# Layer 1 of a spatial convolution scan on Trainium2: the third group's up scan and the fourth group's down scan as joint steps of 256 columns

## The chip, the cores and the metric

The kernel runs on one core of one Trainium2 chip. The metric is the device time of one execution in microseconds. It is float32 throughout. Besides the timed runs there is one profiled execution, whose trace is read here; its times are microseconds from the start of its span.

## What is computed

Two layers of the same kind, each `x = x + scan(groupnorm(x))`, on a tensor of 32 images, 48 channels, 64 rows, 128 columns. A scan goes through all rows downwards, then upwards, then through all columns to the right and to the left; each step adds to the next row (or column) a 1-D convolution (5 taps, 48 to 48 channels) of the row just finished.

```python
def step(w, b):
    def f(carry, inp):
        nxt = inp + _conv1d(carry, w, b)
        return (nxt, nxt)
    return f
xs = jnp.moveaxis(x, 2, 0)
_, d_rest = jax.lax.scan(step(down_w, down_b), xs[0], xs[1:])      # down
D = jnp.concatenate([xs[0][None], d_rest], 0)
seq = jnp.concatenate([D[Hh - 3::-1], D[Hh - 1:Hh]], 0)
_, u_rest = jax.lax.scan(step(down_w, down_b), D[Hh - 1], seq)     # up
...                                                                # right, left
x = x + _L0_conv_ref(_gn(x), ...)
x = x + _L1_conv_ref(_gn(x), ...)
```

The row steps up and down use the same weights (`down_w`). Images do not depend on one another; within an image a step needs the step before it.

## The kernel before

The 32 images are four groups of eight. `PHASES` lists twelve stages in order: a "rows" stage scans one group down and up, a "cols" stage scans two groups to the right and to the left. The four groups are numbered 0 to 3 in the profile's tile names: `step_12u` is a step's sums in layer 1, group 2, going up; `step_13d` is group 3 going down. The stages that matter here are numbers 8 (layer 1, group 2: 12d, then 12u) and 9 (layer 1, group 3: 13d, then 13u); stage 10 is the first column stage of layer 1 (`step_10r`, `step_10l`).

A row (128 columns of 8 images of 48 channels) lies in the arena in SBUF as three blocks `o` of 128 partitions (eight neighbouring columns times 48 channels make 384 partitions) and 128 elements (16 column blocks times 8 images). `row_step` (through `step`, line 881) makes one row: nine products in the order of `PRODUCTS`, each with its own 128x128 weights (some with 96 or 112 columns of weights), sum up in three PSUM tiles; when the last product of a block is issued, one vector operation (line 903) adds the bias and the row that waits there, and writes the new row over it. The first block is complete after the fifth product, the third after the sixth, the second after the ninth; the next step starts with products of the first and the third block.

The arena has three slots of 32 rows. Stage 8 has rows 0 to 31 in slot 0 and rows 32 to 63 in slot 1; stage 9 has rows 0 to 31 in slot 2 and rows 32 to 63 in slot 1 (`slots`, `row_views`), so its second half is loaded when stage 8 has left slot 1. Rows come from DRAM (`take_rows`, from `mid`, written by layer 0's last stage, by 16 rows), are scaled in place by ScalarE (`scale_rows`: group norm's factor and offset) and go, when finished upwards, to DRAM (`move_rows` to `ups`, tile `upb` in the profile), from where the column stages read them (`load_unit`).

What sets the order: an `agenda` of (time, function) entries, times in steps. `plan_rows` and `plan_cols` fill it, and the last loop runs through the steps of all stages, carrying out before each step what has come due. `in_order` chains instructions of one engine in that order, so an agenda's times set the order in each engine's queue; when something really runs is decided by semaphores that the framework derives from the tiles' accesses. Loads and stores here are all issued by SP, in one queue.

Of the kernel before, what the change touches and what calls it, by code (L numbers as in the profile page):

```python
# [41 lines left out]
GB = 8  # L42
# [35 lines left out]
def weight_runs():  # L78
# [35 lines left out]
    ("cols", 1, 0),  # L114
    ("cols", 1, 1),
)


@with_exitstack
def kernel(  # L120
# [567 lines left out]
    def row_views(k):  # L688
        return [slot[i].rearrange("p (o h n) -> p o h n", o=NG, h=HALF) for i in slots(k)]

    def row(k, h):
        return row_views(k)[h // HALF][:, :, h % HALF]

    def move_rows(k, h0, h1, to_dram, q=None):

        _, layer, g = PHASES[k]
        view = row_views(k)[h0 // HALF]
        t = (ups if to_dram else source)[layer][g]
        for h in range(h0, h1, E8):
            end = min(h1, h + E8)  # L700
            for o in range(NG):
                for e, c0, c1, p0 in pieces(o):
                    here = view[p0 : p0 + c1 - c0, o, h % HALF : h % HALF + end - h]
# [12 lines left out]

    def take_rows(k, h0, h1, o):

        _, layer, g = PHASES[k]
        view = row_views(k)[h0 // HALF]  # L720
        for e, c0, c1, p0 in pieces(o):
            here = view[p0 : p0 + c1 - c0, o, h0 % HALF : h0 % HALF + h1 - h0]
            for q in range(NQ):
                dma(
                    here[:, :, q * RUN : (q + 1) * RUN],
                    by_quarter(source[layer][g], e, h0, h1, q)[c0:c1],
                )

    def scale_rows(k, h0, h1, groups=range(NG)):
        _, layer, g = PHASES[k]  # L730
        scale, offset = coeffs[layer, g]
        view = row_views(k)[h0 // HALF][:, :, h0 % HALF : h0 % HALF + h1 - h0]
        view = view.rearrange("p o h (k b) -> p o b h k", b=GB)
        for o in groups:
            for b in range(GB):
                args = view[:, o, b], scale[:, o, b : b + 1], offset[:, o, b : b + 1]
                nc.scalar.activation(  # L737
                    args[0], args[0], AF.Identity, bias=args[2], scale=args[1]
                )

    def scale_at_once(k, h0, h1, eng, o0=0, o1=NG):

        _, layer, g = PHASES[k]
        view = row_views(k)[h0 // HALF][:, o0:o1, h0 % HALF : h0 % HALF + h1 - h0]
        view = view.rearrange("p o h (k b) -> p o (h k) b", b=GB)
        for t, op in zip(coeffs[layer, g], (ALU.mult, ALU.add)):
            t = t[:, o0:o1].unsqueeze(2).to_broadcast([FULL, o1 - o0, (h1 - h0) * NK, GB])
            eng.tensor_tensor(view, view, t, op)
# [129 lines left out]
                dma(in_output(j, half, e)[c0 * NH : c1 * NH], src[at : at + (c1 - c0) * NH])  # L878


    def step(key, weights, b_at, src, inp, dst, whole, part):


        ps = [
            ps_step.tile([FULL, N], F32, tag=f"step{o}", name=f"step{o}_{key}")
            for o in range(NG)
        ]
        left = [sum(1 for p in PRODUCTS if p[1] == o) for o in range(NG)]
        seen = [0] * NG
        for i, o, s in PRODUCTS:  # L890
            seen[o] += 1
            m = COLUMNS.get((i, o, s), FULL)
            at = FULL * (o - NG * s - i + 1)
            nc.tensor.matmul(  # L894
                part(whole(ps[o])[0:m], -s),
                weights[:, i, at : at + m],
                part(src(i), s),
                start=seen[o] == 1,
                stop=seen[o] == left[o],
            )  # L900
            if seen[o] == left[o]:
                layer, way = b_at
                nc.vector.scalar_tensor_tensor(  # L903
                    dst(o),
                    whole(ps[o]),
                    bd[:, o, layer, way : way + 1],
                    inp(o),
                    ALU.add,
                    ALU.add,
                )  # L910

    def row_step(k, h, prev, inp, name):
        _, layer, g = PHASES[k]

        def part(t, s):
            return t[:, max(0, s) * GB : N + min(0, s) * GB]

        step(
            f"{layer}{g}{name}{h}",
            wt[f"down{layer}"],  # L920
            (layer, DOWN),
            lambda i: prev[:, i],
            lambda o: inp[:, o],
            lambda o: row(k, h)[:, o],
            lambda ps: ps,
            part,
        )

    def col_step(k, way, v0, v1):
        _, layer, pair = PHASES[k]  # L930

        def col(v):
            kb, e = divmod(v, E8)
            j, kk = divmod(kb, KQ)
            view = slot[slots(k)[j % 3]].rearrange(
                "p (o m e k b) -> p o e k m b", o=NG, e=E8, k=KQ, b=GB
            )
            return lambda o: view[:, o, e, kk]

# [4 lines left out]
        step(  # L944
            f"{layer}{pair}{'drl'[way]}{v1}",
            wt["right" if way == RIGHT else "left"],
            (layer, way),
            col(v0),
            col(v1),
            col(v1),  # L950
            lambda ps: ps.rearrange("p (m b) -> p m b", b=GB),
            part,
        )

    def scans(k):
        if PHASES[k][0] == "rows":
            for h in range(1, H):
                yield lambda h=h: row_step(k, h, row(k, h - 1), row(k, h), "d")
            end = last.rearrange("p (o n) -> p o n", o=NG)
            for h in range(H - 2, -1, -1):  # L960
                yield lambda h=h: row_step(
                    k, h, row(k, h + 1), row(k, h - 1) if h else end, "u"
                )
        else:
            for v in range(1, W):
                yield lambda v=v: col_step(k, RIGHT, v - 1, v)
            for v in range(W - 2, -1, -1):
                yield lambda v=v: col_step(k, LEFT, v + 1, v)


    agenda = []
# [14 lines left out]
    def plan_input(g, times, work, lag, nats, perms):  # L986
# [5 lines left out]
        for j, t in enumerate(times):  # L992
# [6 lines left out]
                at(t + i * work / per + 4, put_out, g, rows * j + r, perm)  # L999
            at(t + lag, stats.take_others, pieces_of * j, nat)  # L1000
            if j + ahead < len(times):
                free = t + 7
                at(free, take_in, g, rows * (j + ahead), nat)
        spread(t + work + lag + (0, 2, 32, 5)[g], scaling(f"x{g}", 0, g, stats, x_masks, (0, 0, 8, 0)[g]), 1)

    def plan_rows(k, t0, prev):
        if k == 1:
# [5 lines left out]
        if k:  # L1013
            for i in range(4):
                if PHASES[k][1]:
                    for o in range(NG):
# [8 lines left out]
        seam = following and follows(k + 1)  # L1025
        if seam:
            cuts = cuts[2:]
            end = t0 + 2 * (H - 1)
# [13 lines left out]
        at(  # L1042
            t0 + H - 1,
            nc.gpsimd.tensor_copy,
            last.rearrange("p (o n) -> p o n", o=NG),
            row(k, H - 1),
# [7 lines left out]
    def plan_cols(k, t0, prev):  # L1054
# [5 lines left out]
        for i in range(n):  # L1060
# [93 lines left out]
            store_result(k, 0, i, perm)  # L1154


    starts = [0]
    for kind, *_ in PHASES:
        starts.append(starts[-1] + 2 * ((H if kind == "rows" else W) - 1))
    for k, (kind, layer, _) in enumerate(PHASES):  # L1160
        (plan_rows if kind == "rows" else plan_cols)(k, starts[k], PHASES[k - 1][0])

# [217 lines left out]
            in_order(fn, *args)  # L1380

    for k in range(len(PHASES)):
        for one in scans(k):
            catch_up(done)
            in_order(one)
            done += 1
    catch_up(float("inf"))


# [51 lines left out]
```

## Time and profile before

| what | value |
|---|---|
| three timed runs | 4165.12, 4167.84, 4174.18 us |
| median of them | 4167.84 us |
| profiled execution: its span, first to last instruction (no other time of it is listed) | 4158.1 us |
| median less that span | 9.7 us |
| TensorE busy, share of the span | 97% |
| VectorE / ScalarE / GpSimd busy | 52% / 30% / 20% |
| granted TensorE clock, mean | 0.989 |

How to read it: TensorE's matmuls are pipelined, so the profile's "busy" of an instruction says little about its cost; the distance from one matmul to the next does. An idle engine costs only where the others wait for it. A group's row gives the line of the kernel, the engine, the operation, the tiles written and read, the count, then busy time and mean duration of one, then the idle time ahead of them and what ended it.

### The profile page before, as it was taken

The page shows a single profiled execution, that of the slowest core. Times are in us where ns is not written, and L with a number is a line of the kernel's source. Part 1 is how long each engine was busy: PE and PEld are TensorE (multiplying, and loading weights), DVE is VectorE, ACT ScalarE, POOL GpSimd, SP SyncE. Part 2 cuts the span into 40 slices and gives each one's busy share as a digit, 9 for nine tenths or more (in the row PEclk, how much of TensorE's full clock was granted, in tenths as well). Part 3 has the DMA queues.
Part 4 walks back from the last instruction along what each step waited for, and adds up shares of the span by engine and source line. Part 5 has one row for each costly group of instructions (what it writes and reads, how often), then busy time and mean ns, then how long its engine had stood idle before and what let it go on. Part 6 is the DMA issues. An engine that isn't in the chain of part 4 may idle for free. (4 is left out here: it accounts for less than half of the span.)

```text
span 4158.1 us, 90227 instructions
## 1 busy us (share of the span) xinstructions
PE 4049.2 (97%) x36724; PEld 4031.7 (97%) x36724; DVE 2141.6 (52%) x6503; ACT 1251.6 (30%) x2440; POOL 826.1 (20%) x763
## 2 busy tenths in 40 slices
PE   6999999999999999999999999999999999999994
PEld 5999999999999999999999999999999999999994
DVE  6454444456654454444457664444444444444444
ACT  4645000536964543000006863423000002200122
POOL 5630010334222000010013220000000015610353
PEclk9999999999999999999999999999999999999997
DMA  9987769669979999258419979959289029999799
GB/s 299 229 184 121 116 127 214 209 159 252 218 188 163 173 163 156 35 103 194 107 30 273 181 147 145 141 93 150 49 141 208 1 55 247 295 257 155 146 233 197
DMA packets 2208479, 681.08 MB, mean 164 GB/s; under 512 B 2008656, under 2 KB 2157376, under 8 KB 2183488
## 3 DMA queue, kind: packets, MB, share of 16 engines
q1 hardware_dynamic: 2063936, 582.35, 68.4%
q10 hardware_dynamic: 141568, 87.46, 8.8%
q0 software_dynamic: 2560, 5.51, 0.5%
q8 instruction: 289, 4.73, 0.5%
q14 instruction: 126, 1.03, 0.1%
HBM read 398.29 MB, written 295.14 MB: 167 GB/s over the span
## 5 line engine op out<-in xcount | busy, mean ns | idle before, releaser
L829 POOL TENSOR_TENSOR arena<-arena 128x2048 f32<-128x2048 f32 x80 | 362.7, 4545 | 1481.7 <-PE step_10l L894 458.3
L737 ACT ACTIVATE arena<-arena,offset,scale 128x256 f32<-128x256 f32 (+2 forms) x744 | 538.4, 818 | 384.4 <-DMA arena<-mid 206.1
L674 POOL COPY arena<-arena 128x256 f32<-128x256 f32 x340 | 201.0, 659 | 447.6 <-DMA arena<-in_x 418.2
L612 ACT ACTIVATE early<-arena 128x256 f32<-128x256 f32 x192 | 129.7, 675 | 443.0 <-DMA arena<-xin 308.1
L894 PE MATMUL step_00r<-arena,early 128*128 128x128 f32 x2286 | 252.1, 274 | 6.1 <-DMA arena<-arena 5.1
L894 PEld LDWEIGHTS step_00r<-arena,early 128*128 128x128 f32 x2286 | 251.2, 185 | 7.0 <-issue 5.5
L894 PE MATMUL step_01r<-arena,early 128*128 128x128 f32 x2286 | 252.2, 274 | 5.8 <-DMA arena<-arena 4.9
L894 PEld LDWEIGHTS step_01r<-arena,early 128*128 128x128 f32 x2286 | 251.3, 185 | 6.6 <-issue 5.3
L894 PE MATMUL step_11r<-arena,early 128*128 128x128 f32 x2286 | 249.3, 272 | 0.3 <-DVE arena L903 0.3
L894 PEld LDWEIGHTS step_11r<-arena,early 128*128 128x128 f32 x2286 | 248.7, 184 | 0.8 <-DVE arena L903 0.7
L894 PE MATMUL step_00l<-arena,wleft 128*128 128x128 f32 x2286 | 249.2, 272 | 0.0
L894 PEld LDWEIGHTS step_00l<-arena,wleft 128*128 128x128 f32 x2286 | 248.7, 184 | 0.0
L894 PE MATMUL step_10l<-arena,wleft 128*128 128x128 f32 x2286 | 248.5, 272 | 0.0
L894 PE MATMUL step_11l<-arena,wleft 128*128 128x128 f32 x2286 | 248.5, 272 | 0.0
L894 PE MATMUL step_10r<-arena,early 128*128 128x128 f32 x2286 | 248.4, 272 | 0.0
L894 PE MATMUL step_01l<-arena,wleft 128*128 128x128 f32 x2286 | 248.4, 272 | 0.0
L894 PEld LDWEIGHTS step_10l<-arena,wleft 128*128 128x128 f32 x2286 | 248.4, 184 | 0.0
L894 PEld LDWEIGHTS step_11l<-arena,wleft 128*128 128x128 f32 x2286 | 248.4, 184 | 0.0
L894 PEld LDWEIGHTS step_01l<-arena,wleft 128*128 128x128 f32 x2286 | 248.4, 184 | 0.0
L894 PEld LDWEIGHTS step_10r<-arena,early 128*128 128x128 f32 x2286 | 248.4, 184 | 0.0
L297 ACT COPY early<-arena 128x1 f32<-128x1 f32 x2 | 0.4, 192 | 709.9 <-DVE arena L903 709.9
L851 ACT COPY arena<-arena 128x256 f32<-128x256 f32 x172 | 99.6, 656 | 362.4 <-POOL arena L829 256.3
(202 smaller groups left out, 7088.5 us busy)
## 6 DMA issues: line engine op xcount, KB each, us to landing
xin<-arena SPq DMA_DIRECT2D x94, 512.0 KB, 4.3
arena<-in_x SPq DMA_DIRECT2D x18, 2048.0 KB, 11.4
arena<-xin SPq DMA_DIRECT2D x96, 384.0 KB, 10.9
arena<-mid SPq DMA_DIRECT2D x384, 96.0 KB, 3.1
upb<-arena SPq DMA_DIRECT2D x192, 192.0 KB, 3.9
arena<-upb SPq DMA_DIRECT2D x96, 384.0 KB, 11.8
arena<-xin SPq DMA_DIRECT2D x174, 192.0 KB, 4.3
mid<-arena SPq DMA_DIRECT2D x32, 1024.0 KB, 11.2
```

Of the source, the lines that this page charges most:

```text
L297: fn(*args)
L612: nc.scalar.activation(junk[:, 0:n], view[:, b], AF.Identity, accum_out=self.sum[:, i, j : j + 1])
L674: copy(dst[:, r, q], src[:, r0 + r, q])
L737: nc.scalar.activation(args[0], args[0], AF.Identity, bias=args[2], scale=args[1])
L829: eng.tensor_tensor(unit, unit, nat, ALU.add)
L851: copy(by_w(perm)[:, a], src[:, a])
L894: nc.tensor.matmul(part(whole(ps[o])[0:m], -s), weights[:, i, at : at + m], part(src(i), s), start=seen[o] == 1, stop=seen[o] == left[o],)
```

## The change

Stage 9's down scan no longer follows stage 8's up scan: both run together as 63 joint steps. In joint step `i` group 2 makes row 62 - i (upwards) and group 3 makes row 1 + i (downwards). Both use the same weights, so one product streams both rows: 256 columns (240 for the products across a border) in one matmul, taken from two places of the arena by an access pattern with a far stride (`beside`), into PSUM tiles of twice the width. One vector operation finishes both rows of a block. The last joint step, whose upward row takes its input from a kept copy, uses two. In the agenda a joint step counts as two steps, and stage 9's start moves back over stage 8's up scan.

So that group 3 can run while group 2 is still in slot 1, its rows lie in the arena in blocks of eight in reversed order (`place`): its rows 32 to 39 lie where group 2's rows 56 to 63 were, which are finished first. Each block is loaded once the rows before have been stored: `take_rows` and `scale_rows` for group 3 go by eight rows, 34 and 17 half steps ahead of their use, and group 2's stores go one half step behind the row they need. Stage 10 loads its first quarter 58 instead of 70 steps ahead.

```diff
+JOINED = (9,)
...
+    def rows_at(k, h0, h1):
+        places = sorted(place(k, h) for h in range(h0, h1, E8))
+        at = places[0] * E8 + h0 % E8
...
-    def step(key, weights, b_at, src, inp, dst, whole, part):
+    def step(key, weights, b_at, src, inp, dst, whole, part, turn=lambda t: t):
         ps = [
-            ps_step.tile([FULL, N], F32, tag=f"step{o}", name=f"step{o}_{key}")
+            ps_step.tile([FULL, 2 * N], F32, tag=f"step{o}", name=f"step{o}_{key}")
...
-                part(whole(ps[o])[0:m], -s),
+                part(turn(whole(ps[o]))[0:m], -s),
                 weights[:, i, at : at + m],
-                part(src(i), s),
+                part(turn(src(i)), s),
...
+                to, sums, term = dst(o), whole(ps[o]), inp(o)
+                todo = [(to, sums, term)]
+                if isinstance(term, tuple):
+                    todo = [(to[:, c], sums[:, c], term[c]) for c in range(len(term))]
+                for to, sums, term in todo:
+                    nc.vector.scalar_tensor_tensor(
+                        to, sums, bd[:, o, layer, way : way + 1], term, ALU.add, ALU.add
+                    )
...
+    def beside(a, b):
+        shift = b.offset - a.offset
+        assert a.ap == b.ap and shift > 0
+        return bass.AP(a.tensor, a.offset, [a.ap[0], (shift, 2), *a.ap[1:]])
...
+            lambda i: both(row(ku, hu + 1), row(kd, hd - 1), i),
+            inp,
+            lambda o: both(row(ku, hu), row(kd, hd), o),
...
+        if k in JOINED:
+            for i in range(H // E8):
+                h, t = i * E8, t0 + 2 * i * E8
+                for o in range(NG):
+                    at(t - 34 + 2 * o, take_rows, k, h, h + E8, o)
+                at(t - 17, scale_rows, k, h, h + E8)
...
-            t = t0 + 2 * (H - 1) - h0
+            t = t_up + up * (H - 1 - h0)
             if k == 0:
                 t += 16 if h0 >= HALF else 68
+            elif up == 2:
+                t += 1
             elif not following:
-                t = t0 + 92 + 5 * (H - h1) / E8 + (34 if h1 <= HALF else 0)
+                t = t_up + 29 + 5 * (H - h1) / E8 + (34 if h1 <= HALF else 0)
             at(t, move_rows, k, h0, h1, True)
...
-                early = 30 if after else 46 if k == 2 else 70
+                early = 30 if after else 46 if k == 2 else 58 if k - 1 in JOINED else 70
```

What this makes of the engines' queues stands in the built programs. In their rows a number behind a tile's name tells the tiles apart, the sizes at the end are those of the operand written. TensorE first, the third to the eighth product of group 2's first step upwards, before:

```order
L894 MATMUL step2_12u62_24965<-arena_72,early_73 96x120
L894 MATMUL step0_12u62_24963<-arena_72,early_73 96x120
L894 MATMUL step0_12u62_24963<-arena_72,early_73 128x128
L894 MATMUL step2_12u62_24965<-arena_72,early_73 128x128
L894 MATMUL step1_12u62_24964<-arena_72,early_73 128x128
L894 MATMUL step1_12u62_24964<-arena_72,early_73 112x128
```

and the same place now, where `12u62d1` is group 2's row 62 together with group 3's row 1:

```order
L917 MATMUL step2_12u62d1_25121<-arena_72,early_73 96x15x2x8
L917 MATMUL step0_12u62d1_25119<-arena_72,early_73 96x15x2x8
L917 MATMUL step0_12u62d1_25119<-arena_72,early_73 128x16x2x8
L917 MATMUL step2_12u62d1_25121<-arena_72,early_73 128x16x2x8
L917 MATMUL step1_12u62d1_25120<-arena_72,early_73 128x16x2x8
L917 MATMUL step1_12u62d1_25120<-arena_72,early_73 112x16x2x8
```

The products, their order and their weights are the same; the width went from 128 to 16x2x8 and from 120 to 15x2x8 elements. Group 3's own nine products for row 1, which stood 63 steps further on, are gone.

VectorE, with the semaphores that an instruction waits for in brackets (`DMAHW0` to `DMAHW7` count DMAs that have landed, the others what an engine has finished): group 2's rows 55 and 54 upwards, before:

```order
L903 SCALAR_TENSOR_TENSOR arena_72<-step0_12u55_25080,bd_75,arena_72 128x128 [waits PE_49]
L903 SCALAR_TENSOR_TENSOR arena_72<-step2_12u55_25082,bd_75,arena_72 128x128 [waits DVE_49,PE_49]
L903 SCALAR_TENSOR_TENSOR arena_72<-step1_12u55_25081,bd_75,arena_72 128x128 [waits DVE_49,PE_49]
L903 SCALAR_TENSOR_TENSOR arena_72<-step0_12u54_25095,bd_75,arena_72 128x128 [waits PE_49]
L903 SCALAR_TENSOR_TENSOR arena_72<-step2_12u54_25097,bd_75,arena_72 128x128 [waits DVE_49,PE_49]
L903 SCALAR_TENSOR_TENSOR arena_72<-step1_12u54_25096,bd_75,arena_72 128x128 [waits DVE_49,PE_49]
```

and the joint steps of rows 55 and 8, 54 and 9, and the first two operations of 53 and 10 now:

```order
L931 SCALAR_TENSOR_TENSOR arena_72<-step0_12u55d8_25248,bd_75,arena_72 128x2x128 [waits DMAHW3_49,DMAHW4_49,DMAHW2_49,DMAHW5_49,DMAHW1_49,DMAHW6_49,DMAHW0_49,DMAHW7_49,PE_49,Activation_49]
L931 SCALAR_TENSOR_TENSOR arena_72<-step2_12u55d8_25250,bd_75,arena_72 128x2x128 [waits DMAHW3_49,DMAHW2_49,DMAHW4_49,DMAHW1_49,DMAHW5_49,DMAHW0_49,DMAHW6_49,DVE_49,DMAHW7_49,PE_49,Activation_49]
L931 SCALAR_TENSOR_TENSOR arena_72<-step1_12u55d8_25249,bd_75,arena_72 128x2x128 [waits DVE_49,PE_49]
L931 SCALAR_TENSOR_TENSOR arena_72<-step0_12u54d9_25313,bd_75,arena_72 128x2x128 [waits DMAHW4_49,DMAHW3_49,DMAHW5_49,DMAHW2_49,DMAHW6_49,DMAHW1_49,DMAHW7_49,DMAHW0_49,PE_49]
L931 SCALAR_TENSOR_TENSOR arena_72<-step2_12u54d9_25315,bd_75,arena_72 128x2x128 [waits DVE_49,PE_49]
L931 SCALAR_TENSOR_TENSOR arena_72<-step1_12u54d9_25314,bd_75,arena_72 128x2x128 [waits DVE_49,PE_49]
L931 SCALAR_TENSOR_TENSOR arena_72<-step0_12u53d10_25340,bd_75,arena_72 128x2x128 [waits PE_49]
L931 SCALAR_TENSOR_TENSOR arena_72<-step2_12u53d10_25342,bd_75,arena_72 128x2x128 [waits DVE_49,PE_49]
```

Rows 55 and 54 waited for TensorE and VectorE alone. Now group 3's row 8, the first of a newly loaded block, brings DMA semaphores and ScalarE's (which scales the block) to step 55; and the first operation of step 54 has DMA semaphores without ScalarE's. The same stands at steps u46d17, u38d25, u30d33, u22d41, u14d49 and u6d57, each one step behind the place where group 2 has finished eight rows.

SP, around group 2's first store (`upb2`, ten DMAs for eight rows) and the loads of group 3 (`arena<-mid3`), before:

```order
L286 DMA arena_72<-mid3_86 16x16x32 x4
L286 DMA arena_72<-mid3_86 48x16x32 x8
L286 DMA arena_72<-mid3_86 32x16x32 x4
L286 DMA upb2_93<-arena_72 48x32x32 x2
L286 DMA upb2_93<-arena_72 32x32x32
L286 DMA upb2_93<-arena_72 16x32x32
L286 DMA upb2_93<-arena_72 48x32x32 x2
L286 DMA upb2_93<-arena_72 16x32x32
L286 DMA upb2_93<-arena_72 48x32x32 x2
L286 DMA upb2_93<-arena_72 32x32x32
L286 DMA upb2_93<-arena_72 48x32x32 x2
L286 DMA upb2_93<-arena_72 32x32x32
```

and now:

```order
L287 DMA arena_72<-mid3_86 48x8x32 x8
L287 DMA arena_72<-mid3_86 32x8x32 x4
L287 DMA upb2_93<-arena_72 48x32x32 x2
L287 DMA upb2_93<-arena_72 32x32x32
L287 DMA upb2_93<-arena_72 16x32x32
L287 DMA upb2_93<-arena_72 48x32x32 x2
L287 DMA upb2_93<-arena_72 16x32x32
L287 DMA upb2_93<-arena_72 48x32x32 x2
L287 DMA upb2_93<-arena_72 32x32x32
L287 DMA arena_72<-mid3_86 16x8x32 x4
L287 DMA arena_72<-mid3_86 48x8x32 x8
L287 DMA arena_72<-mid3_86 16x8x32 x4
```

Before, loads of group 3's rows 0 to 31 (by 16 rows) end, and then the stores of rows 56 to 63, 48 to 55 and so on follow one another. Now ten stores stand between loads of eight rows each: the stores of rows 56 to 63 come behind loads for group 3's rows 24 to 31, and the rest of that block's loads behind them.

More of the change, by code (lines that the diff above doesn't have):

```diff
@@ L700, in move_rows @@
             end = min(h1, h + E8)
+            view = rows_at(k, h, end)
             for o in range(NG):
                 for e, c0, c1, p0 in pieces(o):
-                    here = view[p0 : p0 + c1 - c0, o, h % HALF : h % HALF + end - h]
+                    here = view[p0 : p0 + c1 - c0, o]
                     if to_dram:
@@ L719, in take_rows @@
         _, layer, g = PHASES[k]
-        view = row_views(k)[h0 // HALF]
+        turned = h1 - h0 > E8 and place(k, h0) > place(k, h0 + E8)
+        if turned:
+            for h in range(h0, h1, E8):
+                take_rows(k, h, h + E8, o)
+            return
+        view = rows_at(k, h0, h1)
         for e, c0, c1, p0 in pieces(o):
-            here = view[p0 : p0 + c1 - c0, o, h0 % HALF : h0 % HALF + h1 - h0]
+            here = view[p0 : p0 + c1 - c0, o]
             for q in range(NQ):
@@ L924, in row_step, with lines, two_row_step, both @@
             lambda o: row(k, h)[:, o],
-            lambda ps: ps,
+            lambda ps: ps[:, 0:N],
             part,
+        )
+    def beside(a, b):
+        shift = b.offset - a.offset
+        assert a.ap == b.ap and shift > 0
+        return bass.AP(a.tensor, a.offset, [a.ap[0], (shift, 2), *a.ap[1:]])
+    def lines(t):
+        return t.rearrange("p (m b) -> p m b", b=GB)
+    def two_row_step(ku, hu, kd, hd):
+        _, layer, g = PHASES[ku]
+        first = slots(ku)[0] < slots(kd)[0]
+        def both(u, d, o):
+            u, d = lines(u[:, o]), lines(d[:, o])
+            return beside(*((u, d) if first else (d, u)))
+        def inp(o):
+            if hu:
+                return both(row(ku, hu - 1), row(kd, hd), o)
+            pair = lines(last.rearrange("p (o n) -> p o n", o=NG)[:, o]), lines(row(kd, hd)[:, o])
+            return pair if first else pair[::-1]
+        def part(t, s):
+            return t[:, max(0, s) : NK + min(0, s)]
+        step(
+            f"{layer}{g}u{hu}d{hd}",
+            wt[f"down{layer}"],
+            (layer, DOWN),
+            lambda i: both(row(ku, hu + 1), row(kd, hd - 1), i),
+            inp,
+            lambda o: both(row(ku, hu), row(kd, hd), o),
+            lambda ps: ps.rearrange("p (c m b) -> p c m b", c=2, b=GB),
+            part,
+            lambda t: t.rearrange("p c m b -> p m c b"),
         )
@@ L1001, in plan_input @@
             if j + ahead < len(times):
-                free = t + 7
-                at(free, take_in, g, rows * (j + ahead), nat)
-        spread(t + work + lag + (0, 2, 32, 5)[g], scaling(f"x{g}", 0, g, stats, x_masks, (0, 0, 8, 0)[g]), 1)
+                at(t + 7, take_in, g, rows * (j + ahead), nat)
+        t += work + lag + (0, 2, 32, 5)[g]
+        spread(t, scaling(f"x{g}", 0, g, stats, x_masks, (0, 0, 8, 0)[g]), 1)
     def plan_rows(k, t0, prev):
+        down, up = (2 if k in JOINED else 1), (2 if k + 1 in JOINED else 1)
+        t_up = t0 + down * (H - 1)
         if k == 1:
@@ L1027, in plan_rows @@
             cuts = cuts[2:]
-            end = t0 + 2 * (H - 1)
+            end = t_up + up * (H - 1)
             at(end - E8, move_rows, k, E8, 2 * E8, True, 0)
@@ L1154, in last_results @@
             store_result(k, 0, i, perm)
-    starts = [0]
-    for kind, *_ in PHASES:
-        starts.append(starts[-1] + 2 * ((H if kind == "rows" else W) - 1))
+    starts, end = [], 0
+    for k, (kind, *_) in enumerate(PHASES):
+        n = (H if kind == "rows" else W) - 1
+        starts.append(end - 2 * n if k in JOINED else end)
+        end = starts[-1] + (2 if k in JOINED else 1) * n + (2 if k + 1 in JOINED else 1) * n
     for k, (kind, layer, _) in enumerate(PHASES):
@@ L1382 @@
     for k in range(len(PHASES)):
-        for one in scans(k):
+        for units, one in scans(k):
             catch_up(done)
             in_order(one)
-            done += 1
+            done += units
     catch_up(float("inf"))
```

50 lines of the change are left out of this document (27 added, 23 removed).

## The prediction

> **What bounds the kernel now.** I read the page's head and its busy times first, then the stages of layer 1's third and fourth row phases (windows), then the matmuls by form.
>
> ```profile
> span 4158.1 us, 90227 instructions
> PE 4049.2 (97%) x36724; PEld 4031.7 (97%) x36724; DVE 2141.6 (52%) x6503; ACT 1251.6 (30%) x2440; POOL 826.1 (20%) x763
> ```
>
> TensorE and its weight loads are busy 97% of the span; nothing else passes 52%. So a change pays only where it makes TensorE's stream denser, and costs wherever TensorE waits. Now the two stages that the change joins, 12u (third group up) and 13d (fourth group down), and 13u after them:
>
> ```profile
> core 0: us, PE busy (x) PEld busy (x) DVE busy (x) ACT busy (x) POOL busy (x), PEclk, DMA share, GB/s
> 2733.30:2857.80 124.50, 124.50 (x1137) 124.50 (x1136) 60.65 (x190) 34.41 (x46) 0.50 (x1) 1.00 0.69 109
> 2857.80:2983.00 125.20, 125.20 (x1136) 124.75 (x1135) 60.89 (x190) 1.95 (x3) 0.00 (x0) 1.00 0.55 95
> 2983.00:3107.50 124.50, 124.50 (x1137) 124.50 (x1136) 60.64 (x190) 0.00 (x0) 0.51 (x1) 1.00 0.69 117
> ```
>
> 63 steps take 124.5 us, 1.976 us each: nine products of two instructions, 109.8 ns apart. TensorE idles nowhere, the granted clock is 1.00, and weight loading fills the whole stretch as well. 13d's extra 0.7 us are its waits for loaded rows. The two stages take 124.5 + 125.2 = 249.7 us; that is all the change can touch directly.
>
> **The change, part by part: the matmuls.** 63 joint steps of nine products take the place of 126 steps: half the weight loads, products twice as wide. Does a wide product cost less than two narrow ones? Nothing here has 256 columns, so I bound it by the rows of 128 and of 512 columns.
>
> ```profile
> L894 PE MATMUL step_12u<-arena,early x1134: 266/275/304, 2733.4 to 2857.8; 128*128 128x128 f32 x126, 128*96 128x120 f32 x63
> L1299 PE MATMUL rows<-arena,wleft x40: 592/592/1222, 19.6 to 38.1; 128*128 128x512 f32 x40
> 23.60:37.50 13.90, 13.90 (x34) 6.19 (x33) 1.00 1.01 417
> ```
>
> From 128 to 512 columns an instruction lasts 592 - 275 = 317 ns longer, 0.826 ns a column, so 128 columns stream in 106 ns of the 109.8 ns pace. In the window of 512-column products the weight loads are busy 6.19 of 13.90 us, against all of the time in the steps: wide products hide their weight loads. A 256-column product thus needs 211 ns an instruction (everything beyond the streaming hidden) to 219.6 (nothing gained). I take 215.5, the streaming plus the 4 ns left over now, since at 512 columns the pace is 13.90/33 = 421 ns, no better than streaming alone; for the border products (240 columns) 202. A joint step is then 14 x 0.2155 + 4 x 0.202 = 3.83 us, 63 of them 241 us: **8 us less** than 249.7 (bounds 0 and 13). Eight blocks of loaded rows instead of four in 13d add about another 0.7 us of such waits: net 7.
>
> **The wait that the change adds.** The VectorE rows shown above carry the case. In the joint scan the first vector operation of steps u54d9, u46d17, u38d25, u30d33, u22d41, u14d49 and u6d57 waits for DMA semaphores on top of TensorE; for u30d33 the second one does, too. Before, no step of 12u or 13u waits for a DMA. What are these DMAs? Not the fourth group's rows: those are waited for at u55d8, with ScalarE's semaphore (they are scaled there), and at u54d9 ScalarE is not waited for. What stands on SP just ahead is the ten stores of third-group rows 56 to 63, which SP can issue only once the row above them is done. One vector operation now writes two rows that lie 11392 to 13184 elements apart (`beside`), and the stored rows lie between the two in the arena; I read the wait as the framework guarding the span between the rows, not as a value that is needed. It is in the program whatever its reason, and it repeats every eight steps, seven times.
>
> What is queued behind it: VectorE's two other operations of that step, and through them TensorE's next step, whose first product reads what the waiting operation writes. Behind TensorE waits the whole kernel. What the store takes comes from 13u, where the same ten stores run alone:
>
> ```profile
> L286 SPq DMA_DIRECT2D upb<-arena x10: 302/842/1362, 3028.2 to 3036.0; - x10
> DMA to landing us min/median/max: 2.9/3.7/4.2
> ...
> 3028.00:3030.00 2.00, 2.00 (x21) 2.00 (x20) 0.99 (x4) 0.00 (x0) 0.00 (x0) 1.00 0.41 72
> 3030.00:3039.00 9.00, 9.00 (x85) 9.00 (x84) 4.65 (x15) 0.00 (x0) 0.00 (x0) 1.00 1.00 161
> 3039.00:3040.00 1.00, 1.00 (x12) 1.00 (x11) 0.28 (x2) 0.00 (x0) 0.00 (x0) 1.00 0.03 4
> ```
>
> Issues from 3028.2 to 3036.0, the last one landing 3.7 us later: 11.5 us, during which the 16 DMA engines are full. In 13u nobody waits for it; TensorE is busy throughout. Bounds from the stores that run in a queue of 40, and from their fastest rows:
>
> ```profile
> L286 SPq DMA_DIRECT2D upb<-arena x40: 433/774/2287, 2634.0 to 2673.7; - x40
> DMA to landing us min/median/max: 3.0/3.9/5.4
> L903 DVE SCALAR_TENSOR_TENSOR arena<-step_12u,bd,arena x186: 341/351/352, 2734.7 to 2856.1; 128x128 f32<-128x128 f32 x186
> ```
>
> Ten at 0.774 us and 3.0 to land make 10.7; ten at 39.7/39 = 1.02 us and 3.9 make 14.1. Set 0 where the first joint step ahead of the wait ends on TensorE. Its first bank is finished four products earlier (8 x 0.2155 = 1.7 us); with the matmul's own latency (275 ns + 106) and the vector operation, the first store issues at about -1.0. The vector operation over 256 columns lies between 0.351 (as now) and 0.702 (two of the present ones); I take 0.5, and it adds little either way. The last store lands at -1.0 + 11.5 = 10.5, the waiting operation ends at 11.0, and TensorE starts the next step there instead of at 3.83. **Stall 7.2 us**, seven times: 50 (from 10.7: 45; from 14.1: 68).
>
> **The clock.** Such a stall is long enough to lower TensorE's clock. Three stalls in this trace are alike; one with its surroundings, and the resumptions after the other two:
>
> ```profile
> 1850.34 2.01 PE L894 MATMUL step_01r<-arena,early 128*128 128x128 f32 x7 [4.92 <-DMA arena<-arena]
> ...
> 1845.30:1850.30 5.00, 0.12 (x2) 0.00 (x0) 0.35 (x1) 0.00 (x0) 0.00 (x0) 0.88 0.10 14
> 1850.30:1855.90 5.60, 5.56 (x25) 5.41 (x26) 1.05 (x3) 0.00 (x0) 0.00 (x0) 0.50 0.10 14
> 1855.90:1861.50 5.60, 5.60 (x53) 5.60 (x52) 2.77 (x9) 0.00 (x0) 0.00 (x0) 1.00 0.09 12
> 577.40:582.80 5.40, 5.40 (x25) 5.22 (x26) 1.05 (x3) 0.00 (x0) 0.00 (x0) 0.50 0.10 14
> 1181.30:1186.90 5.60, 5.51 (x26) 5.55 (x27) 1.29 (x4) 5.38 (x15) 0.17 (x1) 0.50 1.04 365
> ```
>
> After 4.92 us of waiting the clock stands at 0.50 for the next 5.6 us, in which 25 matmuls issue instead of 53: 2.8 us lost. In the stall itself it was low for 0.24 x 5.0 = 1.2 us, 6.8 in all. If the low stretch is as long after a 7.2 us stall, some 3.4 us of it fall behind the stall, 1.7 lost; if it lasts as long after the work resumes, 2.8. I take 2.1 each, 15 us in all (12 to 20). [...]
>
> **What stays hidden.** The fourth group's loads become 320 of 8 rows instead of 160 of 16, all on SP, in the same queue as the stores.
>
> ```profile
> L286 SPq DMA_DIRECT2D arena<-mid x80: 303/527/2032, 2675.2 to 2724.6; - x80
> ...
> 2685.53 6.05 ACT L737 ACTIVATE arena<-arena,offset,scale 128x256 f32<-128x256 f32 x8 [43.56 <-DMA arena<-mid]
> ```
>
> Eighty loads take 49.4 us here, 0.62 us each with their queue; half the rows cost no more, so one block of eight rows is at most 40 x 0.62 = 25 us of SP, and with ten stores 36. Eight joint steps with one stall last 8 x 3.83 + 7.2 + 2.1 = 40 us, so SP keeps up, and each block is asked for 15 to 17 steps ahead of its use. ScalarE's scaling of a block is three times 6.05 us at most, 18 us, in the same 40. The first block: from 2634.0, 20 stores (20 us), its 40 loads (25), 10 more stores between them (10) and the scaling (18) end at 2707, ahead of 2733.3. If this cover fell away, a late block would cost what SP exceeds 40 us by, seven times. The column phase behind loads its first quarter 58 instead of 70 units ahead, 115 us before it is read: no cost.
>
> **Sum.** -7 + 50 + 15 = +58 us. The profiled span of 4158.1 becomes 4216; the median of the runs shown is 9.7 us above that span (4167.84), and I put the same 9.7 us on top: **4226 us**, 1.4% slower.
>
> **Rivals.**
> 1. No stall: if the semaphore values named are those of the loads, which landed long before, the vector operation never waits and the change gives -7 us: 4161. It decides by which DMA was counted last. For it: the rows name a semaphore, not a value. Against it: the wait stands exactly one step behind each eight-row edge of the rows going up, and without ScalarE's. [...] Chance 6%, of it 2% a gain of over 0.2%, 4% within (0.2%, 8 us, is about what a measurement of this kernel can tell from no change).
> 2. A short stall: stores that land within about 5 us, as a single one does (3.7 us after its issue), would hold TensorE some 1 us and leave the clock up: -7 + 7 = 4168. It decides at the DMA engines' rate; the row of 161 GB/s at share 1.00 says they are the limit, so 2%.
> 3. SP becomes the bound: if a load of eight rows holds SP longer than 0.75 us, the block and its stores pass 40 us and each edge gets later still; at 1 us, 10 us more at each of seven: 4296. The issue times above (0.527 median) speak against it: 6%.
> 4. The forecast: 86%.
>
> The range goes from +40 (45 of stall and 8 of clock, the gain at 13) to +83 (68 and 20, the gain at 5): 4208 to 4251, and leaves out rivals 1 to 3 and some of the forecast's edges, about 2 in 10. Faster 0.02, same 0.06, slower 0.92.
>
> **What the changed kernel's profile will show.** Matmuls of 256 columns about 215 ns apart (step 1 is right if a step without a wait takes 3.8 to 3.85 us). Seven gaps on TensorE in some 300 us, about 38 to 42 us apart, and VectorE's idle time there ended by the DMA that writes the third group's store buffer `upb`. PEclk at 0.5 behind each gap. If the gaps are missing, rival 1 holds; if they are ended by `mid` loads or ScalarE, rival 3. If the gaps are there but the clock stays at 1.00, the time is near 4211.

## The result and the profile after

The changed kernel takes **4235.57 us** (median of 5 runs, 4229.78 to 4238.76) against 4167.84: ratio 1.0159, 95% interval [1.0147, 1.0170], 1.6% slower. That is 10 us above the forecast of 4226 and inside its range.

The page of the profile after the change, its head, busy times and two rows of its slices:

```profile
span 4237.1 us, 88135 instructions
PE 4063.6 (96%) x35590; PEld 4003.7 (94%) x35590; DVE 2107.9 (50%) x6317; ACT 1279.3 (30%) x2536; POOL 826.5 (20%) x763
...
PE   6999999999999999999999999987899999999994
...
PEclk9999999999999999999999999998999999999997
```

TensorE has 1134 instructions fewer and yet a longer busy time, and in three slices (27th to 29th, some 320 us) the engine is no longer full; the clock's row drops in one of them, the 28th. Cut by stage and by one of the gaps (columns: stretch, length, busy time and instructions of each engine, granted clock, DMA share, GB/s), the windows of the changed kernel read:

```profile
2749.70:2784.10 34.40, 34.40 (x164) 29.49 (x163) 11.71 (x26) 12.55 (x24) 0.50 (x1) 1.00 0.34 54
2784.10:2791.60 7.50, 0.39 (x2) 0.00 (x1) 0.54 (x2) 0.00 (x0) 0.00 (x0) 0.79 0.86 138
2791.60:2797.00 5.40, 5.40 (x17) 4.34 (x18) 1.64 (x4) 0.00 (x0) 0.00 (x0) 0.66 0.52 81
2797.00:2802.00 5.00, 5.00 (x25) 4.31 (x24) 1.88 (x4) 3.94 (x8) 0.00 (x0) 1.00 0.54 84
...
2749.70:3061.40 311.70, 259.71 (x1137) 217.32 (x1136) 87.73 (x192) 71.14 (x136) 0.50 (x1) 0.90 0.40 64
```

The last row is the whole joint stage: 311.7 us where the two stages of before took 249.7. TensorE idles 311.7 - 259.7 = **52.0 us** of it. The rows above are one of seven such places: nine steps without a gap and the clock at 1.00; 7.5 us with hardly an instruction; then 5.4 us in which 17 matmuls issue where 25 fit in 5.0 us afterwards, at a mean clock of 0.66. The groups of the matmuls by step (last columns: busy us, mean ns, idle us before them and who ended it), three with a gap and one without:

```profile
L917 PE MATMUL step_12u53d<-arena,early 128*128 128x256 f32 x12 | 4.2, 487 | 7.1 <-DVE arena L931 7.1
L917 PE MATMUL step_12u13d<-arena,early 128*128 128x256 f32 x12 | 4.7, 533 | 8.0 <-DVE arena L931 8.0
L917 PE MATMUL step_12u29d<-arena,early 128*128 128x256 f32 x12 | 5.0, 538 | 7.8 <-DVE arena L931 7.8
L917 PE MATMUL step_12u52d<-arena,early 128*128 128x256 f32 x12 | 3.1, 379 | 0.0
```

(The profile drops the digits behind `d`; `12u53d` is step u53d10.) The gaps stand at the first product of steps 53, 45, 37, 29, 21, 13 and 5, each ended by VectorE. What VectorE waited for at the first of them, by the instructions that belong to its tile, and the ten stores beside it:

```profile
L917 PE MATMUL step_12u54d<-arena,early x18: 366/379/379, 2780.5 to 2784.1; 128*128 128x256 f32 x12, 128*96 128x240 f32 x4, 128*112 128x256 f32 x2
L931 DVE SCALAR_TENSOR_TENSOR arena<-step_12u54d,bd,arena x3: 474/474/483, 2791.1 to 2791.9; 128x256 f32<-128x256 f32 x3
its engine sat idle before it (us, times) until:
  DMA arena<-mid: 9.9, 1
...
L287 SPq DMA_DIRECT2D upb<-arena x10: 302/699/1688, 2779.5 to 2787.1; - x10
...
DMA to landing us min/median/max: 2.8/3.7/3.9
```

The stores issue from 2779.5 to 2787.1 and the last lands 3.8 us later, at 2790.9; VectorE starts at 2791.06 and TensorE goes on at 2791.60. But the view names another DMA, a load of group 3 (`arena<-mid`). SyncE issues such loads right behind the stores, and the first of them lands at 2791.2, when VectorE is already at work. Over the whole stage the waits view splits in the same way:

```profile
DVE arena L931 <- DMA arena<-mid: 48.0, 6, 10.2
...
DVE arena L931 <- DMA upb<-arena: 26.0, 3, 10.8
```

So by name six of the nine waits are for loads. But at step 14 (and at step 6) no load lands near the end of the wait, the view names the stores, and the gap is as long as the others:

```profile
L931 DVE SCALAR_TENSOR_TENSOR arena<-step_12u14d,bd,arena x3: 475/476/484, 2994.9 to 2995.7; 128x256 f32<-128x256 f32 x3
its engine sat idle before it (us, times) until:
  DMA upb<-arena: 10.8, 1
```

The built program agrees: at steps 54, 46, 38, 30, 22, 14 and 6 every DMA count that VectorE waits for is the count of a store to `upb2`, none that of a load. The name in the view is that of a neighbour in the queue. The runs below test it.

### The profile page after: what moved, and what is told of

Same layout as the page of the kernel before. It is cut to its first block, busy times and chain, and to the rows that moved or that the text cites. A ratio compares the mean times of both kernels' runs of the same rounds, so it can differ in the third digit from the quotient of the medians.

```text
span 4237.1 us, 88135 instructions
## 1 busy us (share of the span) xinstructions
PE 4063.6 (96%) x35590; PEld 4003.7 (94%) x35590; DVE 2107.9 (50%) x6317; ACT 1279.3 (30%) x2536; POOL 826.5 (20%) x763
## 5 line engine op out<-in xcount | busy, mean ns | idle before, releaser
L760 ACT ACTIVATE arena<-arena,offset,scale 128x256 f32<-128x256 f32 (+2 forms) x840 | 565.9, 767 | 459.3 <-DMA arena<-mid 224.4
```

What stands on the lines that cost most here:

```text
L760: nc.scalar.activation(args[0], args[0], AF.Identity, bias=args[2], scale=args[1])
```

## The experiments

In all of them the joint stage's length, TensorE's idle time in it and its busy time beyond 241.3 us (what the stage takes where nothing waits, as in e1; the half clock, added products and slower restarts are in it) come from one windows row, the time from 4 to 12 runs each. The runs of before that stand beside them have medians of 4170.15 (e1 to e4) and 4167.61 us (e5 to e8).

| kernel | time, us | ratio to before [95%] | joint stage | TensorE idle | busy beyond |
|---|---|---|---|---|---|
| the change | 4235.57 | 1.0159 [1.0147, 1.0170] | 311.7 | 52.0 | 18.4 |
| e1 two writes | 4161.13 | 0.9978 [0.9967, 0.9989] | 241.3 | 0 | 0 |
| e2 not joined | 4168.41 | 0.9999 [0.9989, 1.0009] | - | - | - |
| e3 32 products in the gap | 4259.63 | 1.0214 [1.0194, 1.0233] | 337.9 | 0 | 96.6 |
| e4 one step split | 4201.66 | 1.0075 [1.0059, 1.0092] | 281.6 | 26.9 | 13.4 |
| e5 16 products in the gap | 4218.24 | 1.0120 [1.0106, 1.0134] | 298.9 | 5.9 | 51.7 |
| e6 stores two steps later | 4233.52 | 1.0154 [1.0140, 1.0168] | 311.4 | 52.4 | 17.7 |
| e7 stores of four rows | 4160.28 | 0.9982 [0.9973, 0.9990] | 241.2 | 0 | 0 |
| e8 two steps split | 4167.34 | 1.0000 [0.9991, 1.0009] | 245.4 | 2.9 | 1.2 |

### e1: two rows, two writes

```diff
-            if hu:
-                return both(row(ku, hu - 1), row(kd, hd), o)
-            pair = lines(last.rearrange("p (o n) -> p o n", o=NG)[:, o]), lines(row(kd, hd)[:, o])
+            up = row(ku, hu - 1) if hu else last.rearrange("p (o n) -> p o n", o=NG)
+            pair = lines(up[:, o]), lines(row(kd, hd)[:, o])
             return pair if first else pair[::-1]
```

> Every joint step writes its two rows by two VectorE operations of 128 columns per row block (six a step in place of three); matmuls, order of the steps, loads and stores stay. Theory (VectorE waits because the write of two far rows spans the rows that are being stored, and no value is late): the seven TensorE gaps vanish, the clock stays 1.00 in the joint stage, a joint step takes 3.83 to 3.85 us throughout, the stage 242 us instead of 311.7; time 4236 - 54 (gaps) - 15 (half clock) = 4161 to 4170 us, within 0.2% of before or a little faster. Rival A (the rows wait for the stores by need, or the stores hold up something else): gaps of 7 us stay, 4230 to 4240. Rival B (the six shorter operations are themselves too slow for a step, about 6 x 0.35 us = 2.1 us of 3.83, with the sums' buffer single): 0.2 us more a step, no gaps of 7 us, 4175 to 4185.

The joint stage of e1 in the windows, the matmuls of a step that had a gap, and its six vector operations:

```profile
2740.10:2981.40 241.30, 241.30 (x1136) 206.88 (x1135) 110.03 (x377) 71.15 (x136) 0.50 (x1) 1.00 0.51 82
...
L917 PE MATMUL step_12u53d<-arena,early 128*128 128x256 f32 (+2 forms) x18 | 4.0, 376 | 0.0
...
L931 DVE SCALAR_TENSOR_TENSOR arena<-step_12u55d,bd,arena 128x128 f32<-128x128 f32 x6 | 1.8, 347 | 2.0 <-PE step_12u55d L917 1.9
```

No gap, clock 1.00, 241.3 us: the theory's numbers. Rival A's gaps are not there. Rival B falls with it, since VectorE is busy 1.8 us of each 3.83 and the step gets no longer. The loads, the stores' number and size and the matmuls are those of the changed kernel; only the form of the write differs. e1 beats the changed kernel by 74 us and the one of before by about 9.

### e2: nothing joined

```diff
-JOINED = (9,)
+JOINED = ()
```

> The list of joined phases is empty, so that every step is a single one as before, while the sums' tiles keep the doubled width and the helper functions their new form. Theory (all of the loss lies in the joint stage): the time of before, 4160 to 4176, and stage 12d starts at 2608 us. Rival (the doubled tiles cost something ahead of the joint stage, where the profile after the change is 16.5 us later): 4180 to 4190 and a start of 12d at 2620 to 2626.

This kernel isolates the doubled tiles of the sums. Stage 12d, the last ahead of the joint stage, lies in the profiles of before, of the change, of e2 and of e1 at:

```profile
L894 PE MATMUL step_12d<-arena,early x1134: 266/275/377, 2608.1 to 2733.3; 128*128 128x128 f32 x126, 128*96 128x120 f32 x63
```

```profile
L917 PE MATMUL step_12d<-arena,early x1134: 266/275/377, 2624.6 to 2749.7; 128*128 128x128 f32 x126, 128*96 128x120 f32 x63
```

```profile
L917 PE MATMUL step_12d<-arena,early x1134: 266/275/377, 2616.1 to 2741.2; 128*128 128x128 f32 x126, 128*96 128x120 f32 x63
```

```profile
L917 PE MATMUL step_12d<-arena,early x1134: 266/275/377, 2614.9 to 2740.0; 128*128 128x128 f32 x126, 128*96 128x120 f32 x63
```

The start moves between 2608 and 2625 us while the stage itself takes 125.2 us or 125.1 in each. e2's start, 2616.1, is neither the theory's 2608 nor the rival's 2620 to 2626, but its time decides: 0.9999 of before, to within 4 us. The wide tiles cost nothing that can be measured. One profiled execution differs from the next by up to 16.5 us ahead of the joint stage, so the 79 us between the two spans is not the effect of the change; the 62 us between the joint stages is (behind them the two kernels differ by 0.6 us).

### e3 and e5: TensorE kept busy in the gap

```diff
...
+        if warm:
+            spare = ps_rows.tile([FULL, BN], F32, tag="rows0", name=f"warm_{key}")
+        for _ in range(warm):
+            nc.tensor.matmul(
+                spare[:, 0 : 2 * N], weights[:, 0, 0:FULL], weights[:, 0, 0 : 2 * N], start=True, stop=True
+            )
         for i, o, s in PRODUCTS:
...
+            32 if hu % E8 == 5 and hu < 54 else 0,
```

> Ahead of the first product of steps 53, 45, 37, 29, 21, 13 and 5 TensorE issues 32 products of 256 columns (32 x 0.2155 = 6.9 us) from the weights into a spare tile that nobody reads, so that it works through the 7.6 us in which VectorE waits; they add work and leave the results as they are. Theory (the waits cost 54 us and the half clock that follows idleness another 15): VectorE's waits stay, the granted clock stays 1.00, the time falls by 12 to 18 us to 4218 to 4224. Rival (the half clock doesn't come from idleness, or the dummy products delay the stage): 4232 to 4245.

The windows of e3, the whole joint stage and the stretch of one set of extra products, and VectorE's waits for DMAs (74.0 us in the changed kernel):

```profile
2747.10:3085.00 337.90, 337.90 (x1583) 291.95 (x1583) 87.33 (x191) 71.15 (x136) 0.50 (x1) 1.00 0.37 59
...
2781.60:2795.40 13.80, 13.80 (x65) 12.15 (x65) 1.27 (x3) 0.13 (x1) 0.00 (x0) 1.00 0.68 108
...
DVE arena L937 <- DMA arena<-mid: 49.7, 6, 11.2
DVE arena L937 <- DMA upb<-arena: 25.7, 3, 10.5
```

The time missed both numbers. A product here is two instructions, which the prediction's own count of nine products and 18 instructions says and the sizing of this experiment forgot: 32 products took 13.8 us, outlasted the wait, and the stage became 241.3 + 7 x 13.8 = 337.9 us. The clock, though, is 1.00 throughout, with VectorE waiting as long as ever. e5 has 16 in the place of 32.

> As e3, but with 16 products in place of 32 ahead of steps 53, 45, 37, 29, 21, 13 and 5. In e3 the profile shows each of these products as two instructions of 0.2155 us, so 32 of them took 13.8 us, 6 us more than the wait; 16 take 6.9 us and end within it. Theory (the half clock follows idleness): 0.7 us is left of each gap, the clock stays 1.00 behind them, the joint stage takes 241.3 + 53.5 = 295 us instead of 311.7, the time 4236 - 17 = 4219 (4214 to 4225). Rival (the clock halves because of the wait itself or of the transfers that run then): 4232 to 4240 with the clock at 0.5 behind each gap.

The joint stage of e5 in the windows, and its largest gaps:

```profile
2745.00:3043.90 298.90, 293.02 (x1359) 249.65 (x1358) 87.34 (x191) 71.44 (x137) 0.50 (x1) 0.99 0.42 67
...
L923 PE MATMUL step_12u37d<-arena,early 128*128 128x256 f32 x12 | 4.1, 477 | 2.2 <-DVE arena L937 2.2
L923 PE MATMUL step_12u29d<-arena,early 128*128 128x256 f32 x12 | 3.3, 388 | 1.5 <-DVE arena L937 1.5
```

4218.24 against the expected 4219: 17 us less than the changed kernel, with work added and every wait in its place. Of the 51.7 us of busy time beyond 241.3 the added products are 7 x 6.9 = 48.3, which leaves 3.4 where the changed kernel has 18.4. Only step 37, behind the longest gap (2.2 us), has slowed matmuls: mean 477 ns, against 388 behind the 1.5 us of step 29. The half clock's part of the 3.4 is an estimated 1.7, half of the shortest low stretch in the trace of the change, 3.41 us; the stage's mean clock of 0.99 agrees. By that estimate the rest comes at full clock, as do e8's 1.2 (clock 1.00). So the second term of the loss comes from idleness of TensorE, not from the wait or the transfers.

### e4 and e8: the write split in one step, and in two

```diff
-            if hu:
+            if hu and hu % E8 != 6:
                 return both(row(ku, hu - 1), row(kd, hd), o)
...
```

> Only the steps 62, 54, 46, ... 6, at which VectorE waits, write their rows by two operations; all other joint steps keep the joint write. Theory (any joint write that spans the stored rows waits, whichever step it is in): the wait moves one step on, to u53d10, u45d18 and so on, and is shorter by the 3.83 us of the step between, so seven gaps of 3.8 us: 4236 - 27 = 4209 if the clock still halves behind them, down to 4194 if gaps of 3.8 us leave the clock at 1.00. Rival A (these seven writes alone are guarded): no gaps, 4161 to 4170. Rival B (the wait has nothing to do with the form of the write): seven gaps of 7.6 us, 4230 to 4240.

The matmul groups of e4 with gaps, three of seven:

```profile
L917 PE MATMUL step_12u52d<-arena,early 128*128 128x256 f32 x12 | 3.2, 388 | 3.4 <-DVE arena L931 3.4
L917 PE MATMUL step_12u28d<-arena,early 128*128 128x256 f32 x12 | 4.8, 526 | 4.8 <-DVE arena L931 4.8
L917 PE MATMUL step_12u4d<-arena,early 128*128 128x256 f32 x12 | 5.2, 589 | 3.3 <-DVE arena L931 3.3
```

The gaps moved one step on, from 53 to 52 and so on, and shrank from 7.1 to 8.0 us to 3.3 to 4.8: the step that now runs ahead of the wait takes 3.83 us of it. The next joint write waits in place of the split one, so it is any far write, not those seven. Behind five of the seven gaps the matmuls are still slowed (mean 513 to 589 ns in place of 379; the stage's mean clock is 0.95), not behind those of steps 52 and 44 (388). In e8 two steps are split (`hu % E8 not in (5, 6)`).

> As e4, but steps 62, 61, 54, 53, ... 6 and 5 write their rows by two operations. Theory: the wait moves to u52d11, u44d19 and so on, where e4's gaps of 3.4 to 5.0 us are shorter by another step of 3.83 us: 0 to 1.2 us each, some 3 us in all, no half clock; 4161 to 4170. Rival (each further step keeps a wait of its own, of 3 us or more): 4185 to 4205.

The joint stage of e8 in the windows and its largest gap:

```profile
2737.00:2982.40 245.40, 242.53 (x1135) 206.22 (x1135) 92.97 (x239) 73.14 (x140) 0.50 (x1) 1.00 0.51 82
...
L917 PE MATMUL step_12u27d<-arena,early 128*128 128x256 f32 x12 | 3.3, 388 | 1.9 <-DVE arena L931 1.9
```

No step split, one, two, all: 52.0, 26.9, 2.9, 0 us of idle time. The store's landing stays where it is and the wait is what is left of it when the next far write comes up. (Step 27's 1.9 us is the one beyond the expected 1.2.)

### e6: the stores later in the queue

```diff
             elif up == 2:
-                t += 1
+                t += 5
```

> The stores of each eight finished rows of group 2 stand two joint steps later in SyncE's queue (7.7 us); everything else stays, joint writes included. Theory (the joint writes and the stores are ordered both ways by a guard on the form of the write, since no value is late): the stores wait for the joint write of step 53 and the write of step 52 waits for the stores, so seven gaps of 7 to 8 us stay and stand two steps later (first products of steps 51, 43, 35, 27, 19, 11 and 3): 4228 to 4242. Rival (a store waits only for the rows that it reads, so that it starts two steps ahead of its place): the gaps shrink to 0 to 1 us, 4161 to 4172.

Two matmul groups of e6 and the first ten stores of group 2:

```profile
L917 PE MATMUL step_12u51d<-arena,early 128*128 128x256 f32 x12 | 4.1, 476 | 7.4 <-DVE arena L931 7.4
L917 PE MATMUL step_12u43d<-arena,early 128*128 128x256 f32 x12 | 4.6, 520 | 7.4 <-DVE arena L931 7.4
...
L287 SPq DMA_DIRECT2D upb<-arena x10: 303/710/1593, 2780.1 to 2787.6; - x10
```

The gaps went with the stores: steps 51 and 43 in place of 53 and 45, as long as before. The first store issues 2780.1 - 2742.7 = 37.4 us into the joint stage, against 2779.5 - 2749.7 = 29.8 in the changed kernel: 7.6 us later, two steps, although the rows that it reads were finished at the same point as before and SyncE had issued nothing since 2771.7. So the guard works both ways: the store, too, waits for the last far write ahead of it, which touches none of its rows (in the built program the first store waits for step 53's vector operation, in the changed kernel for step 55's, in the kernel before for that of row 56, the last row it reads). Only stores were moved, and the gaps went with them: the loads that the waits view names do not set them.

### e7: half the rows in a store

```diff
+        if up == 2:
+            cuts = list(range(0, H + 1, E8 // 2))
         for h0, h1 in zip(cuts, cuts[1:]):
```

> Group 2's finished rows are stored in joint steps as four rows a transfer in place of eight: 20 stores of half the size per eight steps, each set at the end of its four rows; joint writes stay. In the program the joint writes then wait for none of these stores. Theory (the wait on the stores alone made the gaps): no gaps, 4161 to 4172. Rival A (SyncE, which issues 88 transfers per eight joint steps, becomes the bound with 10 more): the blocks of group 3 come later and later, gaps at the first step of a block, 4175 to 4300. Rival B (the joint write by itself is late whenever transfers run): gaps of some us stay, over 4190.

The joint stage of e7 in the windows, VectorE's waits for DMAs, and the page's list of DMA issues in that stretch (KB each, median us to landing):

```profile
2743.30:2984.50 241.20, 241.20 (x1136) 206.81 (x1135) 88.58 (x191) 74.09 (x142) 0.50 (x1) 1.00 0.54 87
...
DVE arena L931 <- DMA arena<-mid: 5.2, 3, 1.8
DVE arena L931 <- DMA upb<-arena: 5.0, 3, 1.7
...
upb<-arena SPq DMA_DIRECT2D x92, 96.0 KB, 2.4
arena<-mid SPq DMA_DIRECT2D x135, 48.0 KB, 2.0
```

With the joint writes in place, the same bytes stored and about twice as many stores, the gaps are gone, and the longest wait of VectorE for a DMA is 1.8 us, hidden behind TensorE. SyncE carries the extra issues without making anything late. (They are 60 per eight steps, 40 loads and 20 stores, not the expectation's 98.) This run has no wait on a store of group 2 in its program: every DMA count that VectorE waits for behind the first joint step is that of a load, so the three waits that the view puts down to stores are again a neighbour's name. The joint write waits for stores of eight rows (the change, seven steps) and for none of four, and in either case it touches none of the stored rows. Why that is so wasn't settled.

## Why the prediction was right, point by point

- **Matmuls**, 3.83 us a step and 241 us for 63: e1 and e7 take 241.3 and 241.2 us, and e3's 64 added instructions of 256 columns 13.8 us, 215.6 ns each where 215.5 was taken; 8.4 us are gained. The 0.7 us put on for loaded blocks did not come: TensorE idles nowhere in e1 and e7. The reading that it rested on isn't shown either, since in 13d before VectorE's idle time ended on TensorE, 63.8 us of it, and on no load.
- **The wait**, 7 x 7.2 = 50 us: 52.0. First store, landing and restart came within 0.2 us of the forecast: at the first gap the stores issue 1.0 us ahead of step 54's first product (2780.5; forecast 1.0), take 11.4 us to the last landing (11.5), and TensorE is back 11.1 us behind that product (11.0). The later gaps are up to 0.9 us longer than the first. The vector operation over 256 columns takes 0.48 us (0.5 taken).
- **What the wait is.** "Not a value that is needed" is shown: e1 and e7 drop it without a value coming earlier. "The framework guarding the span between the rows" is too simple, since in e7 four stored rows lie in the same span without a guard.
- **The clock**, 15 us: 18.4 (20 was the upper bound; the range's low end took 8 where the lower bound was 12, which decided nothing). Of these 18.4 the half clock itself makes an estimated 16.6, half of the 33.2 us that TensorE was busy in the trace's low stretches. e5 shows that its cause is idleness: 5.9 us of it there and a mean clock of 0.99 in the joint stage, against 52.0 and 0.90. The low stretches in the trace of the change last 6.8 us at the first two gaps and 10.2 at the others, the wait's own part included; the term was taken from three stalls of about 5 us and low stretches of 6.8 us, and missed the longer ones. In the traces of before and the change the low stretches from 100 to 4100 us, three and twelve, start on one grid of 3.413 us each, to within 0.01 us, and last 1 to 3 times as long. The length of a gap alone doesn't decide: behind e4's 3.3 us at step 4 the matmuls take 589 ns in the mean, behind its 3.4 and 3.3 us at steps 52 and 44 they take 388.
- **What stays hidden** stayed hidden; rival 3 (SyncE as the bound) falls with e7, where SyncE issues more still. Rival 1's number, 4161, is what e1 and e7 gave: it priced the change without its wait correctly. It falls because the counts waited for are those of the stores, which the built program could have shown before any run. One sign did not come as forecast: VectorE's idle time was to be ended by the DMA that writes `upb`, and `mid` loads were to mean rival 3. By name the loads have six of nine waits and 48.0 of 74.0 us, so the view alone would have spoken for rival 3.
- **The sum.** The joint stage gave +62.0 where +58 was forecast. The measured +67.7 (interval 61 to 71) contains it. Carrying the 9.7 us between span and median over was a step of another kind than the prediction put it: 1.7 us lie around each span (4238.76 - 4237.1 in the changed kernel), and the other 8 were a profiled run of before that was fast ahead of the joint stage, as e2 shows.

## What to carry to other kernels

Merging two operations into one with a far-apart pair of rows can cost more than it saves, since here the framework made the joint write wait for stores of rows that it doesn't touch (52.0 us of TensorE's time, against 8.4 saved), and not the two writes of e1 (0): look in the built program for semaphores that the merged instruction waits for and the separate ones did not, find the transfer behind each by the count that is waited for, and price its landing, not its issue. Where the wait is false, writing the two rows apart (six vector operations of 0.35 us a step, off the path) or storing in smaller pieces took it away here; both gave 4160 to 4161 us, 0.2% under the kernel of before. And price a stall of TensorE at more than its length: here 52 us of waiting cost 70.

## What had not been expected of the hardware

- The prediction took its low stretches from stalls of about 5 us; shorter gaps lower the clock, too, but not all of them. The traces of before and the change have 17 gaps of over 1.5 us between the starts of matmuls behind the first 100 us. Laid on the grid of 3.413 us that the starts of the low stretches give (idleness counted from 0.2 us after the last start), the fifteen that fill 0.65 or more of any one step of the grid are followed by 0.5; three of these, of 2.74, 4.13 and 4.49 us from issue to issue, fill no step whole (0.74, 0.82 and 0.65). The one that fills 0.55, 2.06 us, leaves the clock at 1.00. The last, the second half of the gap at step 29, came while the clock was low already. In e5 2.2 us at step 37 are followed by slowed matmuls (mean 477 ns), in e4 3.4 us at step 52 are not (388): that the place on the grid makes this difference is the author's estimate and was not shown in those two.
- A store of half the size landed 2.4 us after its issue in e7 (median of its largest group, 96 KB), against 3.8 for the 192 KB stores of the change.
- Ahead of the joint stage, executions of kernels that do the same there differ by up to 16.5 us (12d starts at 2608.1 us before, at 2624.6 in the change); between 500 and 1900 us the trace of the change has five stretches of half clock, 34.1 us in all, that of before three, 20.5 us.
